# Two steps moved in the outputs stage of a mixture-of-experts kernel: one sum on VectorE, one small projection on TensorE

## The chip, the cores and the metric

The kernel runs on one core of a Trainium2 chip. The engines named here are TensorE (PE; its weight loads are listed apart, as PEld), VectorE (DVE), ScalarE (ACT), GpSimd (POOL) and SyncE (SP), which issues most of the DMAs. Each takes its instructions in the order of its queue and waits for the others at semaphores. The metric is the device time of one execution in microseconds (us), the median of several.

## The reference

Eight sequences `x` of 512 tokens with 256 channels, a context of 64 rows and one anchor row for each sequence. All in fp32.

```python
nx = _layer_norm(x, ln_gamma, ln_beta)
q = nx @ Wq;  k = prototype_bank @ Wk;  v = prototype_bank @ Wv
weights = softmax(einsum('bth,bph->btp', q, k) * H ** (-0.5))
evidence = einsum('btp,bph->bth', weights, v)
combined = concatenate([nx, evidence, anchor], axis=-1)
router_probs = softmax(combined @ router_W + router_b)
h = silu(einsum('btc,ecr->bter', combined, e_w1) + e_b1)
expert_out = einsum('bter,erh->bteh', h, e_w2) + e_b2
routed = sum(expert_out * router_probs[..., None], axis=-2)
g = sigmoid(silu(combined @ gate_w1 + gate_b1) @ gate_w2 + gate_b2)
return x + g * (routed @ out_w + out_b)
```

There are three experts with 512 hidden channels each. `prototype_bank` is the context and `anchor` the broadcast anchor row.

## The kernel before

The eight sequences are worked in four pairs `j` = 0 to 3. A pair goes through `gate_layer` (the first layer of the gate), `expert_layer` for each of the three experts (the first layer of the experts) and `outputs` (the second layer of the gate, then that of the experts). The order of the instructions on each engine is the order in which the program writes them; no scheduler changes it. Work for the next pair is put into this order at named points: the main loop fills the dictionaries `within` and `between` with steps, and `run(point)` in a stage calls the steps of that point.

The products are arranged after Strassen's scheme: the two sequences of a pair and two blocks of channels are the 2 x 2 blocks, and seven products with sums and differences of blocks stand in for eight. So an operand is often a difference that VectorE makes in place, and a result is added up from several PSUM banks. A product is 128 x 512 in fp32 and is listed as two matmuls. `product` (L796) issues it; `experts` issues six of them, one for each pair of hidden blocks, into one bank.

`outputs(j)` begins with the gate. Its products stand in this order on PE: `u` (L1032), `z` (L1033), `y` (L1038), `u` (L1039), `z` (L1043), `u` with `t3` (L1045). In the traces their banks are `ps_gu`, `ps_gz` and `ps_gy`. After the third, fifth and sixth, `gate` adds a bank to a part kept earlier (L1025, VectorE) and takes the sigmoid (L1027, ScalarE). The parts are copied out of the banks by L1035, L1036 and L1040 on ScalarE; the last of these is the copy of `u` that must be done before the sixth product writes on into `u`.

Then `run("begin")` (L1047) calls the steps for the next pair, where there is one: loads of `x`, `transpose_blocks` (L628 on VectorE, the scaling L570 on ScalarE), `value_weights(j + 1, E)`, which multiplies `v` by the gate's and router's part of the first layer (four small matmuls of L771 into `ps_vw`, and the copy L778 to `vw` on ScalarE), `store_router_rows` (L415) and `spread_router_rows` (L423), four DMAs of POOL's queue that pass the router's rows of `vw` through DRAM. `weigh(j, 99)` multiplies the last hidden blocks by the router's probabilities (L880) and takes their differences (L876), on VectorE. `run("gate")` loads the next xg through SP's queue (L475).

Four bias sums follow (L1077 on ScalarE, L1082 on VectorE), and then the second layer of the experts:

- `experts(u, a(q, 0, 0))`, the last gate product L1143 and `keep(r11, u)`. `keep` adds a bank to a result (L1088, VectorE).
- `experts(z, combo(S1), 0, 1)`, the fifth product set in Strassen's count, into the bank `z`.
- `subtract((0, 1), ...)` and `subtract((0, 0), ...)`: two sets of three differences (L1072, VectorE, 128 x 1024 each). The first set overwrites what the product set before it read.
- `keep(r22, z)`, then `run("P5")` with the transposes of the next pair's second block.
- `experts(u, combo(S2), 0, 1)`, the sixth set, which reads the first set of differences, and `keep(r12, u)`.
- In pairs 0 to 2: the product set into `y` (finished by L1102), the next pair's scores (`ps_s`, L649), the set that reads the second differences, and `experts(z, combo(S4), 1, 1)`. In pair 3 the S4 set comes directly after the S2 set, into the same bank `z`.

Of the kernel before, what the change touches and what calls it, by code (L numbers as in the profile page):

```python
# [16 lines left out]
def kernel(  # L17
# [55 lines left out]
    E, C3, RH = e_w1.shape  # L73
# [24 lines left out]
    def bank(i, name):  # L98
        return psum.tile([P, 512], F32, tag=f"b{i}", name=name)
# [117 lines left out]
    S1, S2, S4 = range(3)  # L217
# [576 lines left out]
    def product(ps, lhsT, rhs, start=False):  # L794

        nc.tensor.matmul(ps, lhsT, rhs, start=start, stop=True, skip_group_check=not start)  # L796
# [211 lines left out]
    def outputs(j, steps):  # L1008
        last = j == NP - 1

        def run(point):
            for step in steps.get(point, ()):
                step()
# [9 lines left out]
        def gate(k, i, src, part=None):  # L1023
            if part is not None:
                nc.vector.tensor_tensor(hg[k][i], src, part, ALU.add)  # L1025
                src = hg[k][i]
            nc.scalar.activation(hg[k][i], src, AF.Sigmoid, bias=gb2_c[:, k : k + 1])  # L1027
# [3 lines left out]
        u, z, y = (bank(i, f"ps_g{n}_{j}") for n, i in (("u", 0), ("z", 2), ("y", 4)))  # L1031
# [9 lines left out]
        finish_odd(j, PAIRS[-1])  # L1041
        gate(0, 0, g1, y)
        product(z, gw2s[:, S4, :], b22)  # L1043
        gate(0, 1, g2, z)
        product(u, gw[1][0], t3)  # L1045
        gate(1, 1, g22, u)
# [10 lines left out]
        def experts(ps, lhs, k, i, start=False):  # L1057
            for q in range(NQ):
                product(ps, lhs(q), hidden(j, q, k, i), start=start and q == 0)

        def combo(s):
            return lambda q: w2s[:, s, q, :]

        def subtract(dst, other):

            (k, i), (k2, i2), (k3, i3) = dst, *other
            for e in range(E):
                d, p, m = (
                    S["h", ii, e].rearrange("p (q k) t -> p q k t", k=2)[:, :, kk, :]
                    for kk, ii in ((k, i), (k2, i2), (k3, i3))  # L1070
                )
                nc.vector.tensor_tensor(d, p, m, ALU.subtract)  # L1072

        def bias_sum(role, i, row):

            r = work.tile([P, T], F32, tag=role, name=f"{role}_{j}", bufs=1)
            nc.scalar.activation(  # L1077
                by_side(r), pb[:, row, :, 1, :], AF.Identity, bias=b2o[:, i, 0:1],
                scale=b2o[:, i, 1:2],
            )  # L1080
            for e in range(2, E):
                nc.vector.scalar_tensor_tensor(  # L1082
                    by_side(r), pb[:, row, :, e, :], b2o[:, i, e : e + 1], by_side(r), ALU.mult, ALU.add
                )
            return r

        def keep(r, ps):
            nc.vector.tensor_tensor(r, r, ps, ALU.add)  # L1088
# [38 lines left out]
        def finish_tokens(r, ps, i, row):  # L1127
# [9 lines left out]
        r11, r22, r12, r21 = (  # L1137
            bias_sum(f"r{i + 1}{row + 1}", i, row) for i, row in ((0, 0), (1, 1), (0, 1), (1, 0))
        )
        ug = u  # L1140
        u, y, z = (bank(i, f"ps_{n}2_{j}") for i, n in ((1, "u"), (3, "y"), (5, "z")))
# [4 lines left out]
        run("P1")  # L1146
        experts(z, combo(S1), 0, 1, start=True)
        subtract((0, 1), ((1, 1), (0, 1)))
        subtract((0, 0), ((0, 1), (0, 0)))
        keep(r22, z)  # L1150
        run("P5")
        experts(u, combo(S2), 0, 1)
        keep(r12, u)
# [58 lines left out]
    with tc.manual_schedule(engines=None):  # L1212
# [62 lines left out]
        for j in range(NP):  # L1275


            within, between = {}, {}

            def put(where, n, step, *args):  # L1280
                where.setdefault(n, []).append(lambda: step(*args))
# [44 lines left out]
            if j + 1 < NP:  # L1326
                b0, b1 = 2 * j + 2, 2 * j + 3
                if j + 2 < NP:
                    put(between, "begin", load_x, b0 + 2)
                    put(between, "begin", load_x, b1 + 2)  # L1330
                put(within, (0, "A" if j else "D"), statistics, b0, 0, NT)
                if j == 0:
                    put(within, (0, "D"), statistics, b1, 0, NT)
                for i in range(2):
                    put(within, (0, "D") if j else (1, "S"), deviation, j + 1, i)
                for b in (b0, b1):
                    put(within, (1, "W" if j else "S"), normalize, b)
                    put(within, (1, "W" if j else "S"), store_x, b)
                put(within, (1, "C"), regroup_x, b0)
                put(within, (1, "A" if j else "B"), router_part, b0)  # L1340
                put(within, (1, "D" if j else "B"), router_part, b1)
                put(between, "begin", transpose_blocks, b0)
                put(between, "gate", regroup_x, b1)
                put(between, "begin", value_weights, j + 1, E)
                put(between, "begin", store_router_rows, j + 1)
                put(between, "begin", spread_router_rows, j + 1)
                put(between, "P5", transpose_blocks, b1)
                put(between, "P2", scores, j + 1)
                put(between, "P2", combine_x, j + 1, nc.gpsimd)
                put(between, "P7", softmax, j + 1)  # L1350
                put(between, "P7", value_weights, j + 1, 0)
                put(between, "P7", router_logits, j + 1)
                put(between, "P3", turn_weights, j + 1)
                put(between, "P3", router_exp, j + 1)
            gate_layer(j, within)
            for e in range(E):
                expert_layer(j, e, within)
            outputs(j, between)


# [32 lines left out]
```

## Time and profile before

| what | value |
|---|---|
| median of 3 runs | 463.61 us (463.35 to 463.65) |
| the profiled execution | 463.56 us |
| its span, first to last instruction | 461.4 us |
| PE / DVE / ACT / POOL busy | 456.7 / 364.7 / 214.8 / 100.0 us |
| granted TensorE clock, mean | 0.999 |
| outputs stage of pair 0, 1, 2, 3 begins | 95.9, 202.0, 307.9, 413.8 us |

Busy times are sums over the span. PE's are modelled from pipelined matmuls, so the starts of successive matmuls say more than their lengths: while PE is never kept waiting, two matmuls of 512 columns start 0.43 us apart. Where PE waits for an operand, the wait is listed at the weight load in front of the matmul. The chain of work that ended last is followed back from the last instruction; what is on it sets the time.

### The profile page before, as it was taken

The page shows a single profiled execution, that of the slowest core. Times are in us where ns is not written, and L with a number is a line of the kernel's source. Part 1 is how long each engine was busy: PE and PEld are TensorE (multiplying, and loading weights), DVE is VectorE, ACT ScalarE, POOL GpSimd, SP SyncE. Part 2 cuts the span into 40 slices and gives each one's busy share as a digit, 9 for nine tenths or more (in the row PEclk, how much of TensorE's full clock was granted, in tenths as well). Part 3 has the DMA queues.
Part 4 walks back from the last instruction along what each step waited for, and adds up shares of the span by engine and source line. Part 5 has one row for each costly group of instructions (what it writes and reads, how often), then busy time and mean ns, then how long its engine had stood idle before and what let it go on. Part 6 is the DMA issues. An engine that isn't in the chain of part 4 may idle for free.

```text
span 461.4 us, 4756 instructions
## 1 busy us (share of the span) xinstructions
PE 456.7 (99%) x1457; PEld 210.5 (46%) x1457; DVE 364.7 (79%) x682; ACT 214.8 (47%) x371; POOL 100.0 (22%) x149
## 2 busy tenths in 40 slices
PE   9999999999999999999999999999999999999996
PEld 7544555444444444444444444444444444444455
DVE  2988979969799669869799659878889625797983
ACT  3445683655222666557221576448221456458000
POOL 6357715001181300001072300001062300000020
PEclk9999999999999999999999999999999999999999
DMA  8975587302013326812012235702011570000014
GB/s 282 371 153 135 100 229 124 78 0 46 7 23 45 78 85 137 159 24 46 6 23 30 41 136 116 114 0 46 6 24 23 80 197 0 0 0 1 0 20 71
DMA packets 119400, 35.26 MB, mean 76 GB/s; under 512 B 106044, under 2 KB 116336, under 8 KB 118864
## 3 DMA queue, kind: packets, MB, share of 16 engines
q1 hardware_dynamic: 115168, 26.95, 28.7%
q0 software_dynamic: 2176, 7.17, 4.6%
q10 hardware_dynamic: 2032, 0.85, 0.7%
q8 instruction: 11, 0.18, 0.2%
q14 instruction: 13, 0.11, 0.1%
HBM read 27.56 MB, written 7.39 MB: 76 GB/s over the span
## 4 chain that ended last, share of the span: by engine, by line
PE 95%; DVE 4%; issue 0%
PE ps_u L796 43%; PE ps_z L796 18%; PE ps_y L796 14%; PE ps_vw L771 5%; PE ps_gu L796 3%; PE ps_w2o L501 2%; PE ps_s L649 2%; PE ps_gz L796 1%; DVE h L1072 1%; PE ps_tokens L796 1%; PE ps_wake L294 1%; DVE h L880 1%; PE ps_v L339 1%; PE ps_m L339 1%; PE ps_gy L796 1%; DVE r L1082 0%
## 5 line engine op out<-in xcount | busy, mean ns | idle before, releaser
L880 DVE TENSOR_TENSOR h<-h,pb 128x512 f32<-128x512 f32 x96 | 61.9, 694 | 6.5 <-ACT h L829 6.5
L796 PE MATMUL ps_u<-h,w2o 128*128 128x512 f32 x144 | 64.1, 595 | 0.0
L829 ACT ACTIVATE h<-h,abias 128x512 f32<-128x512 f32 x72 | 49.6, 719 | 12.5 <-DVE h L835 12.0
L796 PE MATMUL ps_u<-nxT,w 128*128 128x512 f32 x112 | 55.3, 604 | 0.0
L796 PE MATMUL ps_z<-wT,vw 64*128 64x512 f32 x104 | 49.5, 605 | 0.0
L1105 POOL TENSOR_TENSOR yb<-yb,xb 128x512 f32<-128x512 f32 x14 | 17.7, 1266 | 143.3 <-DVE yb L1104 114.8
L796 PE MATMUL ps_z<-h,w2s 128*128 128x512 f32 x96 | 42.6, 593 | 0.2 <-DVE r L1088 0.2
L838 ACT COPY h<-ps_u 128x512 f32<-128x512 f32 x48 | 27.9, 582 | 30.2 <-PE ps_u L796 29.8
L796 PEld LDWEIGHTS ps_u<-h,w2o 128*128 128x128 f32 x144 | 27.0, 190 | 32.5 <-issue 29.4
L415 POOL DMA_DIRECT2D vrd<-vw x8 | 5.0, 628 | 137.0 <-ACT vw L778 137.0
L1072 DVE TENSOR_TENSOR h<-h,h 128x1024 f32<-128x1024 f32 x24 | 34.3, 1482 | 0.0
L796 PEld LDWEIGHTS ps_u<-nxT,w 128*128 128x128 f32 x112 | 20.2, 190 | 29.4 <-issue 24.2
L829 ACT ACTIVATE h<-ps_u,abias 128x512 f32<-128x512 f32 x24 | 16.5, 687 | 29.7 <-PE ps_z L796 29.4
L796 PEld LDWEIGHTS ps_z<-h,w2s 128*128 128x128 f32 x96 | 18.2, 190 | 23.5 <-issue 21.8
L796 PE MATMUL ps_z<-T,ws 128*128 128x512 f32 x56 | 28.6, 592 | 0.0
L796 PE MATMUL ps_y<-nxT,w 128*128 128x512 f32 x56 | 28.6, 592 | 0.0
L835 DVE TENSOR_TENSOR h<-h,ps_y 128x512 f32<-128x512 f32 x24 | 16.4, 683 | 15.0 <-PE ps_y L796 14.0
L796 PE MATMUL ps_u<-wT,vw 64*128 64x512 f32 x56 | 27.8, 612 | 0.0
L796 PE MATMUL ps_y<-wT,vw 64*128 64x512 f32 x56 | 27.0, 597 | 0.0
L771 PE MATMUL ps_vw<-w,vT 128*128 128x512 f32 (+1 forms) x64 | 26.9, 543 | 0.0
L796 PE MATMUL ps_u<-T,ws 128*128 128x512 f32 x56 | 26.7, 594 | 0.0
L835 DVE TENSOR_TENSOR h<-h,ps_z 128x512 f32<-128x512 f32 x24 | 16.2, 684 | 13.3 <-PE ps_z L796 13.2
(235 smaller groups left out, 803.2 us busy)
## 6 DMA issues: line engine op xcount, KB each, us to landing
pb<-pd POOLq DMA_DIRECT2D x4, 1536.0 KB, 6.5
xb<-in_x_dram SPq DMA_DIRECT2D x64, 64.0 KB, 2.4
out_dram<-yb SPq DMA_DIRECT2D x56, 64.0 KB, 2.0
w<-in_L_xcond_e_w_dram SPq DMA_DIRECT2D x6, 512.0 KB, 10.2
x<-in_x_dram SPq DMA_DIRECT2D x24, 128.0 KB, 3.2
xd<-x SPq DMA_DIRECT2D x24, 128.0 KB, 2.4
xg<-xd SPq DMA_DIRECT2D x48, 64.0 KB, 2.4
scr_wa<-in_L_xcond_e_w_dram SPq DMA_DIRECT2D x3, 512.0 KB, 12.8
```

What stands on the lines that cost most here:

```text
L339: nc.tensor.matmul(ps, w_sb[:, k, m * P : (m + 1) * P], src[:, k, :], start=(k == 0), stop=(k == KH - 1))
L415: nc.gpsimd.dma_start(S["vrd", j][i].rearrange("e c -> c e"), S["vw", j][row_half(i), R0:])
L501: nc.tensor.matmul(ps[:, d * H : (d + 1) * H], w2T[:, k, (i + d) * P : (i + d + 1) * P], ow_sb[:, k, :], start=(k == 0), stop=(k == KH - 1),)
L649: nc.tensor.matmul(ps[side(i, h), g * NH : (g + 1) * NH], mr[:, k, 2 * j + i, g * TB : (g + 1) * TB], S["nxT", 2 * j + i][:, k, h * NH : ( ...
L771: nc.tensor.matmul(ps, vT[:, k, j * 2 * CT : (j + 1) * 2 * CT], w1[:, KH + k, n0:n1], start=(k == 0), stop=(k == KH - 1),)
L796: nc.tensor.matmul(ps, lhsT, rhs, start=start, stop=True, skip_group_check=not start)
L829: nc.scalar.activation(h, h if src is None else src, AF.Silu, bias=abias[:, c, 2 * j + i : 2 * j + i + 1])
L835: nc.vector.tensor_tensor(h, h, part, ALU.add)
L838: nc.scalar.copy(chunk(n, i, d), part)
L880: nc.vector.tensor_tensor(h, h, S["pb", j][:, i, :, 2 * q // RC, :], ALU.mult)
L1072: nc.vector.tensor_tensor(d, p, m, ALU.subtract)
L1105: nc.gpsimd.tensor_tensor(yb, yb, S["xb", 2 * j + row][:, i, :], ALU.add)
```

## The change

Two steps change places, each within `outputs`; no operation is added or taken away. The sum `keep(r22, z)` on VectorE now stands between the two sets of differences and not behind them, in all four pairs. `value_weights(j + 1, E)` is called at a new point `"S4"`, after the gate's fifth product and ahead of its sum, and so before the product with `t3`; before, it was called at `"begin"`, behind that product, the third sum, its sigmoid and the first transposes. On PE the four matmuls of `ps_vw` change places with the product into `ps_gu`. On ScalarE the copy to `vw` moves from behind the two scalings to between the first and the second sigmoid. The router rows' DMAs keep their place in POOL's queue and wait for that copy. In pair 3 there is no next pair, and `"S4"` is empty.

```diff
@@ -1041,6 +1041,7 @@
         finish_odd(j, PAIRS[-1])
         gate(0, 0, g1, y)
         product(z, gw2s[:, S4, :], b22)
+        run("S4")
         gate(0, 1, g2, z)
         product(u, gw[1][0], t3)
         gate(1, 1, g22, u)
@@ -1146,8 +1147,8 @@
         run("P1")
         experts(z, combo(S1), 0, 1, start=True)
         subtract((0, 1), ((1, 1), (0, 1)))
+        keep(r22, z)
         subtract((0, 0), ((0, 1), (0, 0)))
-        keep(r22, z)
         run("P5")
         experts(u, combo(S2), 0, 1)
         keep(r12, u)
@@ -1341,7 +1342,7 @@
                 put(within, (1, "D" if j else "B"), router_part, b1)
                 put(between, "begin", transpose_blocks, b0)
                 put(between, "gate", regroup_x, b1)
-                put(between, "begin", value_weights, j + 1, E)
+                put(between, "S4", value_weights, j + 1, E)
                 put(between, "begin", store_router_rows, j + 1)
                 put(between, "begin", spread_router_rows, j + 1)
                 put(between, "P5", transpose_blocks, b1)
```

## The prediction

> **What bounds the kernel now.** I read the page first, for the busy shares, the granted clock and the chain that ended last.
>
> ```profile
> PE 456.7 (99%) x1457; PEld 210.5 (46%) x1457; DVE 364.7 (79%) x682; ACT 214.8 (47%) x371; POOL 100.0 (22%) x149
> ...
> PEclk9999999999999999999999999999999999999999
> ...
> PE 95%; DVE 4%; issue 0%
> ```
>
> TensorE (PE) is busy for 99% of the span at full clock, and 95% of the chain is its own work. A change that removes no matmul can only move the time by the small holes in PE's queue. The 4% of VectorE (DVE) in the chain says where such holes are. So I next read the chain in order of time, in the last pair's outputs stage.
>
> ```profile
> 428.32 6.81 DVE h L1072 x6
> 435.13 0.61 DVE r L1088
> 435.74 0.04 issue
> 435.78 5.42 PE ps_z L796 x12
> 441.20 5.15 PE ps_u L796 x12
> ```
>
> Here VectorE runs both sets of differences (L1072, six instructions) and then `keep(r22, z)` (L1088), and PE waits for that sum. Then I read the timelines by engine (start, length, what, and in brackets the idle time before it and its releaser). First PE at the gate of pair 0 and of pair 3, and PE in the experts of pair 0:
>
> ```profile
> 99.39 1.02 PE L796 MATMUL ps_gz<-hg,gw2s 128*128 128x512 f32 x2
> 100.25 1.10 PE L796 MATMUL ps_gu<-g_t,gw_sb 128*128 128x512 f32 x2
> 101.19 1.03 PE L771 MATMUL ps_vw<-w,vT 128*128 128x258 f32 x4
> 102.06 5.31 PE L796 MATMUL ps_u<-h,w2o 128*128 128x512 f32 x12
> ...
> 108.07 5.31 PE L796 MATMUL ps_z<-h,w2s 128*128 128x512 f32 x12
> 113.37 5.42 PE L796 MATMUL ps_u<-h,w2s 128*128 128x512 f32 x12
> 118.62 4.88 PE L796 MATMUL ps_y<-h,w2o 128*128 128x512 f32 x11
> ...
> 417.32 1.02 PE L796 MATMUL ps_gz<-hg,gw2s 128*128 128x512 f32 x2
> 418.18 1.10 PE L796 MATMUL ps_gu<-g_t,gw_sb 128*128 128x512 f32 x2
> 419.12 5.31 PE L796 MATMUL ps_u<-h,w2o 128*128 128x512 f32 x12
> ```
>
> A product is two matmuls 0.43 apart, 0.86 us; a set of six experts is 5.15. Then PE's weight loads, which is where its waits sit; a load normally starts 0.43 before its matmul:
>
> ```profile
> 113.36 0.30 PEld L796 LDWEIGHTS ps_u<-h,w2s 128*128 128x128 f32 x2 [0.81 <-DVE h L1072]
> 218.94 0.19 PEld L796 LDWEIGHTS ps_u<-h,w2s 128*128 128x128 f32 x1 [0.24 <-DVE h L1072]
> 324.83 0.19 PEld L796 LDWEIGHTS ps_u<-h,w2s 128*128 128x128 f32 x1 [0.24 <-DVE h L1072]
> 435.78 0.30 PEld L796 LDWEIGHTS ps_z<-h,w2s 128*128 128x128 f32 x2 [1.02 <-DVE r L1088]
> ```
>
> And VectorE from the last gate sum (L1025) to the first difference:
>
> ```profile
> 101.39 0.69 DVE L1025 TENSOR_TENSOR hg<-g_r,ps_gu 128x512 f32<-128x512 f32 x1 [0.18 <-PE ps_gu L796]
> 112.09 3.49 DVE L1072 TENSOR_TENSOR h<-h 128x1024 f32<-128x1024 f32 x3
> ```
>
> The reader should see one link between them. PE's sixth product set (`experts(u, combo(S2), 0, 1)`) starts on the first difference. In pair 0 it waits for it already; in pairs 1 and 2 its load has the ordinary 0.24 ahead of it but names DVE, so the difference came just in time. From 101.39 to 113.31 VectorE runs 18 instructions back to back, none but the first with an idle time before it: whatever delays the first delays the difference.
>
> **What a late operand costs PE.** Three waits of before give the rule. In pair 0 the load came at 113.36 in place of 112.79 (0.57 late) and the product set that follows started at 118.62 in place of 108.07 + 2 x 5.15 = 118.37: 0.25 lost. In pair 3 the load came at 435.78 in place of 435.00 (0.78 late), and the next set at 441.04 in place of 430.28 + 10.30 = 440.58: 0.46 lost. The gate product of L1045 (`gu`), which waits until L1040 has copied its bank, lost 0.08 in pair 3 with its load at 418.16 in place of 417.75, 0.41 late. So the loss is the lateness less 0.32, which is the lead of the load.
>
> **Part 1, the sum moved (`keep(r22, z)` between the two sets of differences).** It adds and removes nothing: one sum of 0.60 pitch (0.68 long) changes places with three differences of 1.14 pitch. In pairs 0 to 2 it needs the bank of the fifth product, whose last matmul ends at 113.38, and VectorE arrives there at 115.5: no wait is added. The second set ends 0.6 later, near 119.6 in pair 0; PE first reads it with the product set at 125.73, 6 us on, so 0. The transposes of the next x block (L628, 119.51) and `keep(r12, u)` come at the same time as before, since the sum is the same. With the cover of 6 us gone it would cost the 0.6. In pair 3 the order of products is another: `experts(z, combo(S4), 1, 1)` stands directly behind the sixth set and needs this sum. The first three differences end at 431.7, so the sum ends at 432.3 instead of 435.73, ahead of the load's natural 435.00. The hole of 0.46 goes: **-0.46**. Next in line is PE itself, since `keep(r12, u)` ends at 436.3, before the product at 440.58, and sums, stores and the tail behind it follow PE and move with it. Its bounds are 0 and -0.46.
>
> **Part 2, value_weights moved ahead of the product with t3 (pairs 0 to 2; pair 3 has no next pair).** PE gets the four small matmuls (`ps_vw`, 102.06 - 101.19 = 0.87) one product sooner. PE's sum of work is unchanged.
> - Gain on PE: `gu`'s load no longer waits for the copy of L1040, because 0.87 of other work stands before it. From `gz` to `ps_u` pair 3 takes 419.12 - 417.32 = 1.80 where two products are 1.72: 0.08 for each of three pairs.
> - Copy of `vw` on ScalarE: 0.35 long, from behind two scalings (L570) to between the first and the second sigmoid. ScalarE is busy from 100.07 to 109.73 either way, and the scalings and the four bias sums (L1077) stay where they are, at about 104.9 and 106.2, with operands from VectorE at 103.6 and 104.2. 0.
> - The router rows on POOL's queue: two stores (L415) and two loads (L423) start some 2.5 us sooner. They are read first at 139.14 (L709) and were issued by 116.0, so nothing is gained, and no other POOL work stands behind them before the output of the stage. SP's loads of the next xg start after the transposes of L628, 0.86 later, for transposes at 119.5, where landing takes at most 8.2. 0.
> - **The cost.** The third gate sum (`gate(1, 1, g22, u)`) waits for `gu`'s product and heads VectorE's strict order; everything to the differences is queued behind it. It was released at 101.39, 2.00 after `gz`'s start, and in pair 3 also 2.00 after (419.32). For the gate sum after an undelayed product the trace has 1.13 from its first matmul (417.32 to 418.45); 0.86 + 1.13 = 1.99, so PE's wait of 0.08 did not hold it. With `vw` between, it comes 0.86 + 0.87 + 1.13 = 2.86 after `gz`: 0.86 later. Counting from PE's recorded matmul starts (0.87 less the 0.08 saved) it would be 0.79. I take **0.86** and keep 0.79 and 0.87 as ends, as the release is VectorE's own row.
>
> Then PE, pair by pair. Pair 0: the difference ends at 113.31 + 0.86, the load follows at 114.22, natural is 112.79 - 0.08 = 112.71; 1.51 late, 1.19 lost, of which 0.25 was lost before: 1.19 - 0.25 - 0.08 = **+0.86**. Pairs 1 and 2: the first difference starts at 217.64 and 323.53 and takes 1.22, so the loads come at about 219.77 and 325.66 in place of 218.86 and 324.75; 0.91 late, 0.59 lost, less 0.08: **+0.51** each. The later differences come every 1.14, PE needs them every 1.72, so one hole per pair. After it VectorE idles 2.6 to 2.95 before the sum with `ps_y` (L1102), so the delay is not carried on.
>
> Sum: 0.86 + 0.51 + 0.51 - 0.46 = **+1.42 us**. The profiled execution took 463.56 (span 461.4 and about 2.2 around it), 0.05 under the median of 463.61. 463.56 + 1.42 = 464.98, and I say **465.0**. With 0.79 in place of 0.86 it is 464.8; with the hole of pair 3 left as well as the greater delay it is 465.5.
>
> A rule that speaks against the change stands in the Trainium skill, "TensorE: Matmul & The Clock Gate", section "A second HAM failure mode: psum-queue depth-cycling": short idles between groups of matmuls can make the clock gate fall to half rate and back, with windows of about 3.4 us. Worked out from that page, as an estimate, three such windows at half rate would add 3 x 1.7 = 5.1 us, and the sum would be 470.1. The rows here are against it: after the hole at 435.78 the next set still took 5.15, at a granted clock of 0.999 over the run.
>
> **The rivals.**
> - *The delay never reaches PE (so not slower).* If something other than VectorE's queue set the first difference, a gate sum that is 0.86 later would change nothing there. The gains are left: 0.08 in pairs 1 and 2 (pair 0 waits for the same difference, so its 0.08 is lost again) and 0.46: 463.56 - 0.62 = 462.94. The net is 3 x delay - 1.16, so it decides below a delay of 0.39 at the difference. For it: nothing but the habit of slack. Against it: the unbroken row from 101.39 and the named releaser in three pairs. 0.05.
> - *The delay is eaten in part.* With 0.4 to 0.68 left, the net is 0.0 to 0.9, about 464.1: no difference that can be told. For it: VectorE's release is inferred, and PE's own 0.08 shifts are of that size. Against it: pair 3 shows the same 2.00 without `vw`. 0.16.
> - *The sum blocks VectorE.* If `keep(r22, z)` waited in pairs 0 to 2 for the fifth set in its new place, and the second set of differences and the transposes came late for PE's scores (123.86, with scaled blocks ready at 121.76), each pair would lose more. With the holes above, the fifth set ends 2.1 before VectorE arrives; only if VectorE gained that much would it wait, and the scores still have 2.1. A loss of 1 us in each of three pairs on top of the sum gives 468.0. 0.02.
> - *More is late than the difference,* for example ScalarE's scalings or a stretched DVE row beside POOL's earlier queue work, 0.3 per pair: 465.9. Against it: L880 kept its 0.60 pitch beside POOL's issue at 106.63. 0.05.
>
> **How the numbers follow.** The forecast has 0.72, with its own range 464.6 to 465.4. No change that a measurement of this kernel can tell is within 0.2%, that is 0.93 us, up to 464.54. The forecast case and the two dearer rivals are slower, save about 0.01: 0.78. The partial case, that hundredth and most of the absorbed case (462.94 is 0.14% under the median) make 0.20. Faster by more needs 462.68, which only the absorbed case comes near: 0.02. The range from 464.0 to 465.8 leaves out the absorbed case, some of the partial one and the dear tails, less than 2 in 10.
>
> **What would show it.** Right: `ps_vw` between `gz` and `gu`; the third gate sum 2.86 after `gz` in pairs 0 to 2 and 2.00 in pair 3; the load of the sixth set held by DVE h for about 1.5, 0.9 and 0.9; no hole before the S4 set of pair 3, the sum of L1088 ending near 432 plus the shift. Wrong: the difference in its old place relative to PE, or holes that grow at other places such as the scores or the last tokens.

## The result and the profile after

The changed kernel takes 464.72 us (median of 8 runs, 464.67 to 464.94) against 463.51 before (8 runs, 463.35 to 463.65): +1.21 us, a ratio of 1.0026 with a 95% interval of 1.0017 to 1.0034. The profiled execution took 464.94 with a span of 462.8; most of the others had a span of 462.6. Its gate of pair 0 begins 0.14 later than in the kernel before (95.99 against 95.85), ahead of any changed instruction.

The page of the kernel after, busy shares and then the chain that ended last by engine:

```profile
PE 456.1 (99%) x1457; PEld 209.7 (45%) x1457; DVE 365.1 (79%) x682; ACT 214.9 (46%) x371; POOL 100.2 (22%) x149
...
PE 87%; DVE 9%; DMA 1%; issue 1%; SPq 0%; DVEq 0%; ACT 0%
```

The busy times are those of before within 0.8 us and PE is still "99% busy": the page alone hides the loss. VectorE's share of the chain has grown from 4% to 9%. The timeline of PE in pair 0 and, last two lines, in pair 3 (columns: start, length, what, idle time before it and its releaser):

```profile
99.53 1.02 PE L796 MATMUL ps_gz<-hg,gw2s 128*128 128x512 f32 x2
100.39 1.03 PE L771 MATMUL ps_vw<-w,vT 128*128 128x258 f32 x4
101.26 1.02 PE L796 MATMUL ps_gu<-g_t,gw_sb 128*128 128x512 f32 x2
102.11 5.31 PE L796 MATMUL ps_u<-h,w2o 128*128 128x512 f32 x12
107.27 1.02 PE L796 MATMUL ps_gu<-g_t,gw_sb 128*128 128x512 f32 x2
108.12 5.31 PE L796 MATMUL ps_z<-h,w2s 128*128 128x512 f32 x12
114.29 5.42 PE L796 MATMUL ps_u<-h,w2s 128*128 128x512 f32 x12 [0.86 <-DVE h L1073]
...
432.08 5.31 PE L796 MATMUL ps_u<-h,w2s 128*128 128x512 f32 x12
437.23 5.31 PE L796 MATMUL ps_z<-h,w2s 128*128 128x512 f32 x12
```

The weight load of the product with `t3` in pair 0, first in the kernel before, then in the changed kernel:

```profile
100.22 0.30 PEld L796 LDWEIGHTS ps_gu<-g_t,gw_sb 128*128 128x128 f32 x2 [0.65 <-ACT g_r L1040]
...
101.04 0.41 PEld L796 LDWEIGHTS ps_gu<-g_t,gw_sb 128*128 128x128 f32 x2
```

PE's weight loads before the sixth product set in the changed kernel, pairs 0, 1 and 2:

```profile
114.29 0.30 PEld L796 LDWEIGHTS ps_u<-h,w2s 128*128 128x128 f32 x2 [1.69 <-DVE h L1073]
220.62 0.30 PEld L796 LDWEIGHTS ps_u<-h,w2s 128*128 128x128 f32 x2 [1.08 <-DVE h L1073]
326.95 0.30 PEld L796 LDWEIGHTS ps_u<-h,w2s 128*128 128x128 f32 x2 [1.09 <-DVE h L1073]
```

VectorE, the third gate sum and the first difference of pair 0, and the moved sum of pair 3:

```profile
102.32 0.69 DVE L1025 TENSOR_TENSOR hg<-g_r,ps_gu 128x512 f32<-128x512 f32 x1 [0.97 <-PE ps_gu L796]
...
113.02 3.49 DVE L1073 TENSOR_TENSOR h<-h 128x1024 f32<-128x1024 f32 x3
...
433.45 0.68 DVE L1089 TENSOR_TENSOR r<-r,ps_z 128x512 f32<-128x512 f32 x1
```

The wait of 0.65 before the product with t3 is gone in pairs 0 to 2, and with it the 0.08: `gz` to `ps_u` is 102.11 - 99.53 = 2.58, two products of 0.86 and the projection's 0.87 to within 0.01, where it was 2.67. In its place VectorE waits 0.97 for the third gate sum. From this sum to the first difference it runs 18 instructions in pair 0 and 17 in pairs 1 and 2 (one L880 of 0.60 fewer, which is why only pair 0 was late already in the kernel before), and then the sixth product set waits for the difference in all three pairs. In pair 3 the S4 set follows the S2 set (432.08) after 5.15, without a hole.

The program repeats itself from pair to pair, so a difference of starts says what each pair costs. Each column is the time from the first `ps_gu` matmul of a pair's gate to that of the next pair, read from PE's timelines; the fourth is from that matmul of pair 3 to the first `ps_tokens`.

| kernel | pair 0 | pair 1 | pair 2 | pair 3 | sum against before |
|---|---|---|---|---|---|
| before | 106.15 | 105.89 | 105.89 | 40.00 | |
| after | 106.93 | 106.33 | 106.34 | 39.53 | +1.20 |
| sum alone | 106.15 | 105.89 | 105.89 | 39.54 | -0.46 |
| projection alone | 106.94 | 106.33 | 106.34 | 39.99 | +1.67 |
| projection in two halves | 106.50 | 105.90 | 105.89 | 39.54 | -0.10 |
| projection two products sooner | 106.94 | 106.32 | 106.33 | 39.54 | +1.20 |
| copy alone sooner | 106.15 | 105.89 | 105.89 | 39.54 | -0.46 |
| a transpose done twice | 106.90 | 106.30 | 106.30 | 39.53 | +1.10 |
| transposes ahead, projection as before | 105.89 | 105.90 | 105.89 | 39.54 | -0.71 |
| transposes ahead, projection ahead | 105.81 | 105.81 | 105.81 | 39.53 | -0.97 |

The theory: a first difference that comes late costs TensorE its lateness less a lead of 0.32. The rivals: the four matmuls (or their copy) cost by the place they were moved to, whatever VectorE's queue holds; or the moved sum has its own price in pairs 0 to 2.

### The profile page after: what moved, and what is told of

Same layout as the page of the kernel before. It is cut to its first block, busy times and chain, and to the rows that moved or that the text cites. A ratio compares the mean times of both kernels' runs of the same rounds, so it can differ in the third digit from the quotient of the medians.

```text
span 462.8 us, 4756 instructions
## 1 busy us (share of the span) xinstructions
PE 456.1 (99%) x1457; PEld 209.7 (45%) x1457; DVE 365.1 (79%) x682; ACT 214.9 (46%) x371; POOL 100.2 (22%) x149
## 4 chain that ended last, share of the span: by engine, by line
PE 87%; DVE 9%; DMA 1%; issue 1%; SPq 0%; DVEq 0%; ACT 0%
PE ps_u L796 42%; PE ps_z L796 16%; PE ps_y L796 14%; PE ps_vw L771 5%; PE ps_gu L796 3%; DVE h L880 2%; PE ps_w2o L501 2%; PE ps_s L649 2%; PE ps_gz L796 1%; DMA x<-in_x_dram 1%; DVE r L1083 1%; DVE h L876 1%; PE ps_tokens L796 1%; DVE nxT L628 1%; DVE h L1073 1%
## 5 line engine op out<-in xcount | busy, mean ns | idle before, releaser
L880 DVE TENSOR_TENSOR h<-h,pb 128x512 f32<-128x512 f32 x96 | 61.9, 695 | 6.5 <-ACT h L829 6.5
```

Of the source, the lines that this page charges most:

```text
L880: nc.vector.tensor_tensor(h, h, S["pb", j][:, i, :, 2 * q // RC, :], ALU.mult)
```

## The experiments

**The two parts apart.** First the sum alone, on the kernel before:

```diff
         subtract((0, 1), ((1, 1), (0, 1)))
+        keep(r22, z)
         subtract((0, 0), ((0, 1), (0, 0)))
-        keep(r22, z)
```

> The kernel before with the sum alone moved between the two sets of differences; the value projection stays where it was. Theory (a late first difference costs TensorE its lateness less 0.32 us): pairs 0 to 2 unchanged, the hole before the S4 set of pair 3 gone, -0.46 us, about 463.05. Rival (the sum between the sets costs VectorE and what waits for the second set in pairs 0 to 2): no gain or a loss, 463.5 or more.

Measured: 463.08 us against 463.59, ratio 0.9989 (0.9980 to 0.9998). Pairs 0 to 2 keep their times to 0.01 us, pair 3 gets shorter by 0.46. So the sum has no price of its own in pairs 0 to 2, and the rival that gave it one is out.

Then the projection alone, the same diff undone on the kernel after:

```diff
-        keep(r22, z)
         subtract((0, 0), ((0, 1), (0, 0)))
+        keep(r22, z)
```

> The changed kernel with the sum back behind both sets; only the value projection is moved. Theory: +0.79 in pair 0 and +0.44 in pairs 1 and 2, the hole of pair 3 back, +1.67 us against before, about 465.2. Rival (the moved sum carries part of the loss): less than the +1.2 of both parts together.

Measured: 465.33 against 463.59, +1.74, ratio 1.0036 (1.0023 to 1.0049); by pairs +0.79, +0.44, +0.45. The two parts add up: 1.74 - 0.51 = 1.23, against 1.21 for both.

**Is it the matmuls' place or VectorE's queue?** The changed kernel, with VectorE's two transposes and their scalings moved to where VectorE idles, between the first and the second gate sum:

```diff
-                put(between, "begin", transpose_blocks, b0)
...
+                put(between, "S4", transpose_blocks, b0)
                 put(between, "S4", value_weights, j + 1, E)
```

> The changed kernel with the first block's two transposes and scalings taken from behind the third gate sum to the point S4, ahead of the second gate sum, where VectorE idles. The projection still stands before the product with t3, so the third gate sum is as late as in the changed kernel, but 1.22 us of VectorE's queue behind it are gone. Theory: the first difference ends 0.4 us sooner than in the kernel before, no hole is left in pairs 0 to 2; -0.25 in pair 0, -0.08 in each of three pairs, -0.46 in pair 3: -0.95 us, about 462.55. Rival (the four matmuls cost by their place on TensorE or the copy by its place on ScalarE, whatever VectorE's queue holds): as the changed kernel, about 464.7.

Measured: 462.62 against 463.59, ratio 0.9978 (0.9969 to 0.9987), -0.97. The matmuls stand where they stand in the changed kernel, and the third gate sum is as late. VectorE in pair 0 of this kernel:

```profile
98.85 0.69 DVE L1025 TENSOR_TENSOR hg<-g_r,ps_gy 128x512 f32<-128x512 f32 x1 [2.12 <-PE ps_gy L796]
99.46 1.30 DVE L628 STREAM_TRANSPOSE nxT<-xg 128x512 f32<-128x512 f32 x2
100.68 0.65 DVE L1025 TENSOR_TENSOR hg<-g_r,ps_gz 128x512 f32<-128x512 f32 x1
102.23 0.69 DVE L1025 TENSOR_TENSOR hg<-g_r,ps_gu 128x512 f32<-128x512 f32 x1 [0.90 <-PE ps_gu L796]
...
111.75 3.49 DVE L1073 TENSOR_TENSOR h<-h 128x1024 f32<-128x1024 f32 x3
```

and PE:

```profile
108.03 5.31 PE L796 MATMUL ps_z<-h,w2s 128*128 128x512 f32 x12
113.18 5.31 PE L796 MATMUL ps_u<-h,w2s 128*128 128x512 f32 x12
118.33 5.31 PE L796 MATMUL ps_y<-h,w2o 128*128 128x512 f32 x12
```

The transposes fill the 1.03 between the first two gate sums and hold up the second by 0.11 (100.68 - 99.44 = 1.24 after `gz`, against 1.13). The sum still comes 102.23 - 99.44 = 2.79 after `gz`, but the difference starts at 111.75, and the sets follow each other every 5.15. All three pairs now take 105.81. The place of the matmuls costs nothing where VectorE's queue is short enough. This version takes 0.97 us less than the kernel before, 0.2%.

The counter-test: PE's order as before, VectorE alone made late, by doing the first transpose twice on the kernel with the sum moved.

```diff
         for k in range(KH):
+            if b % 2 == 0 and k == 0:
+                nc.vector.transpose(nxT[:, k, :], xg[:, k, :])
             nc.vector.transpose(nxT[:, k, :], xg[:, k, :])
```

> The kernel of the sum alone (TensorE's order as in the kernel before) with the first transpose of the next pair's first block done twice, 0.61 us more on VectorE ahead of the first difference in pairs 0 to 2. Theory: the lateness alone makes the loss, +0.61 in pair 0 and 0.61 - 0.03 - 0.32 = +0.26 in pairs 1 and 2, less 0.46 in pair 3: +0.67 us against before, about 464.2. Rival (the place of the matmuls makes the loss): as the sum alone, about 463.05.

Measured: 464.97 (464.75 to 465.28) against 463.59, +1.38, ratio 1.0029 (1.0019 to 1.0040). The rival's 463.05 is out: a late difference makes the loss with PE's order untouched. The direction is the theory's, but the size is twice the expected +0.67. VectorE's timeline shows where most of the rest comes from:

```profile
102.24 0.70 DVE L629 STREAM_TRANSPOSE nxT<-xg 128x512 f32<-128x512 f32 x1
102.98 1.30 DVE L630 STREAM_TRANSPOSE nxT<-xg 128x512 f32<-128x512 f32 x2
104.21 2.46 DVE L882 TENSOR_TENSOR h<-h,pb 128x512 f32<-128x512 f32 x4
```

The second transpose writes what the first wrote, and starts 0.74 after it where the next starts after 0.61. PE's load for the sixth set comes 114.36 - 99.64 = 14.72 after `gz` where it came 113.36 - 99.39 = 13.97 after it in the kernel before: 0.75 late and not 0.61. With 0.75 of lateness the theory gives 0.75 + 2 x (0.75 - 0.35) - 0.46 = 1.09, and the pairs show +0.75, +0.41, +0.41 and -0.47, which is 1.10. The other 0.28 of the median lies outside these stretches: in the profiled execution the gate of pair 0 begins 0.25 later than before (96.10). This comes from the start of the kernel, ahead of any changed instruction: at 35.01 a sum of VectorE into `T` (L642, L640 in the kernel before) took 1.18 where it took 0.69, and PE's load of `T` waited 0.81 for it. GpSimd had an operation of its own from 35.00 (L236) that in the kernel before ran from 34.39 to 35.03; whether that slowed the sum was not tested, nor whether the other runs, which spread over 0.5 us, have the same.

**Threshold or proportion?** Half of the projection ahead, half in its old place:

```diff
-                put(between, "S4", value_weights, j + 1, E)
+                put(between, "S4", value_half, j + 1)
+                put(between, "begin", value_rest, j + 1)
```

`value_half` issues the matmuls of the first 128 channels, `value_rest` those of the other 128 and the copy.

> The changed kernel with the projection cut in two: the matmuls of its first half of the channels stay before the product with t3, those of the second half and the copy go back behind the third gate sum. TensorE has 0.435 us of it ahead of that product in place of 0.87. Theory (lateness less 0.32 of lead): the sum is 0.435 - 0.08 = 0.36 late; +0.36 in pair 0, 0.36 - 0.03 - 0.32 = 0.01 and so nothing in pairs 1 and 2, -0.46 in pair 3: -0.1 us against before, about 463.5. Rival (the loss grows in proportion to the work put ahead): half of the 1.74 of the projection alone, less 0.46: +0.4, about 464.0.

Measured: 463.35 against 463.56, ratio 0.9997 (0.9988 to 1.0006). The interval doesn't exclude no change, but it leaves out the rival's 1.0009 and the pairs decide: +0.35, +0.01, 0. In pair 1 the load waits 0.65, 0.41 more than the ordinary 0.24, and the pair takes 105.90, 0.09 more than without any hole: as much as the product with t3 gains.

```profile
219.50 0.30 PEld L811 LDWEIGHTS ps_u<-h,w2s 128*128 128x128 f32 x2 [0.65 <-DVE h L1088]
```

So half the work ahead costs less than half: there is a lead, and only what exceeds it counts.

**What the projection brings by itself.** The transposes ahead, the projection behind the product with t3:

```diff
         product(z, gw2s[:, S4, :], b22)
+        run("S4")
         gate(0, 1, g2, z)
...
-                put(between, "begin", transpose_blocks, b0)
+                put(between, "S4", transpose_blocks, b0)
```

(with the sum moved, as in the first diff)

> The sum moved, the projection in its old place behind the product with t3, and the first block's two transposes ahead of the second gate sum. Theory: the difference is 1.2 us sooner, the hole of pair 0 (0.25) and that of pair 3 (0.46) go, the 0.08 before the product with t3 stays in all pairs: -0.71 us, about 462.9; behind the kernel with the projection ahead as well by 0.24. Rival (the projection costs wherever it stands ahead): at or below the 462.6 of that kernel.

Measured: 462.80 against 463.56, -0.76, ratio 0.9985 (0.9976 to 0.9994). Beside the -0.97 with the projection ahead that is 0.21 behind, near the expected 0.24; the pairs show it as 105.89 or 105.90 against 105.81, three times. The runs of the two kernels overlap by 0.04 us, so it is the pairs that carry this.

**The copy's place, and two products instead of one.** The point S4 behind the product with t3:

```diff
-        run("S4")
         gate(0, 1, g2, z)
         product(u, gw[1][0], t3)
+        run("S4")
         gate(1, 1, g22, u)
```

> The changed kernel with the point S4 behind the product with t3 and ahead of the third gate sum: TensorE's order is that of the kernel before, only ScalarE's copy to vw comes sooner, between the second and the third sigmoid. Theory: the copy's place costs and brings nothing, as the sum alone: about 463.05. Rival (the copy ahead of the sigmoids and scalings delays ScalarE's bias sums and what waits for them): above 463.5.

Measured: 463.14 against 463.56, ratio 0.9991 (0.9982 to 1.0000); pairs as with the sum alone. And the point S4 one product sooner:

```diff
         gate(0, 0, g1, y)
+        run("S4")
         product(z, gw2s[:, S4, :], b22)
-        run("S4")
         gate(0, 1, g2, z)
```

> The changed kernel with the projection one product sooner still, ahead of the gate's fifth product, so that the second and the third gate sum are both late. Theory: only the third heads the queue to the first difference, and it is as late as in the changed kernel: about 464.75, the same. Rival (each product it passes costs): about 1.7 more than the changed kernel has over the sum alone, about 466.5.

Measured: 464.81 against 463.56, ratio 1.0027 (1.0017 to 1.0038), the pairs as in the changed kernel to 0.01. Here two gate sums are late. PE's last two gate products and VectorE's sums behind them:

```profile
100.27 1.02 PE L796 MATMUL ps_gz<-hg,gw2s 128*128 128x512 f32 x2
101.13 1.02 PE L796 MATMUL ps_gu<-g_t,gw_sb 128*128 128x512 f32 x2
...
101.40 0.69 DVE L1025 TENSOR_TENSOR hg<-g_r,ps_gz 128x512 f32<-128x512 f32 x1 [1.90 <-PE ps_gz L796]
102.19 0.69 DVE L1025 TENSOR_TENSOR hg<-g_r,ps_gu 128x512 f32<-128x512 f32 x1
```

The second one's delay is taken out of VectorE's idle time; the third starts 102.19 - 98.54 = 3.65 after the gate's fourth product (`u`, L1039), as in the changed kernel (102.32 - 98.67). So neither the copy's place nor the number of products passed has a price. What counts is when the last of the three sums lets VectorE go on.

## Why the prediction was right

Forecast +1.42, measured +1.21. The mechanism is the forecast one, a late gate sum that comes back to PE as a late difference; one term of the sum was too large. By its own steps:

- *The sum moved:* -0.46 forecast; -0.47 in the changed kernel and -0.46 alone. The moved sum of pair 3 ends at 433.45 + 0.68 = 434.13; less the shift of the sixth set (432.08 - 430.28 = 1.80) that is 432.33, where 432.3 was forecast. Nothing in pairs 0 to 2, as forecast.
- *0.08 for the product with t3:* it shows in pairs 1 and 2 when the difference is in time: 105.89 to 105.81.
- *The lateness of the third gate sum:* this is the term that was mis-sized. The prediction took 0.86 by the release of a gate sum 1.13 after its product's first matmul, and kept 0.79, counted from PE's starts, as the low end. Measured is 102.32 - 99.53 = 2.79 after `gz` where the forecast had 2.86, against 2.00 before: 0.79, in all three pairs. What failed is the argument that PE's wait of 0.08 did not hold the sum before. It measured the release behind another product: 1.13 holds for `gz` and `gy`. Behind the product with `t3` the release comes 102.32 - 101.26 = 1.06 after the first matmul when PE doesn't wait, and 1.14 in the kernel before, where it waits 0.08 (101.39 - 100.25). So the 0.08 was part of the old 2.00, and the delay is 0.87 - 0.08 = 0.79. With the projection two products sooner it is the same: 102.19 - 101.13 = 1.06, and 101.40 - 100.27 = 1.13 for `gz`. Why the two products differ by 0.07 stays open.
- *The lead of 0.32:* pairs 1 and 2 cost +0.44 and +0.45 in place of 0.51, pair 0 +0.78 in place of 0.86. The lead itself holds: the loads above waited 1.69, 1.08 and 1.09, so 1.45, 0.84 and 0.85 beyond the ordinary 0.24, and in pair 0 the set after it begins at 119.55 in place of 108.12 + 10.30 = 118.42, 1.13 lost, 0.32 less than the lateness. With 0.79 the prediction's formula gives 0.79 + 0.44 + 0.44 - 0.46 = 1.21. That this meets the measured difference to 0.01 is in part luck: the runs of one kernel spread over 0.3.
- *One hole per pair and nothing carried on:* VectorE idles 2.60 before the sum with `ps_y` in each of pairs 0 to 2, and the pairs' periods add up to the whole.
- *ScalarE's copy, the router rows, the loads of xg:* priced at nothing; the run with only the copy sooner agrees. That the stores of the router rows were issued 2.5 us sooner (104.14 against 106.63 in pair 0) brought nothing that shows.
- *The rule on idle holes and the clock gate,* Trainium skill, "TensorE: Matmul & The Clock Gate", section "A second HAM failure mode: psum-queue depth-cycling": that section describes a kernel that cycles through PSUM banks in each iteration, where PE idles briefly between its groups of matmuls often enough for the clock to go to and fro, and the window of about 3.4 us stands in Part 1 of the page. This case's trace shows nothing of it, with one hole in some 106 us. After the hole of 0.86 in pair 0 the next set took 114.29 to 119.55, 5.26 with its restart, and the mean granted clock of the run was 1.000. Holes so short and so rare did not lower the clock, and the estimate of 470.1 made from that page did not come.

Of the rivals, the absorbed delay is refuted by the releasers of the three loads above, and the blocked VectorE by the run of the sum alone, in which pairs 0 to 2 keep their times. Of more that is late nothing shows: the lateness of the loads less 0.32 accounts for what each pair costs to 0.02. Part of the delay was absent, 0.07 of 0.86; only below 0.70 would the change have fallen within 0.2%.

## What to carry to other kernels

An engine that is 99% busy still waits for others at a few operands; before moving work ahead on it, follow the first result that gets later through the strict queue of the engine that takes it, to the operand that comes back. If that queue runs back to back to the operand, the whole delay comes back, less the lead that the weight load has, here 0.32 us. The remedy can be on the other engine: moving 1.22 us of transposes into VectorE's idle time turned the same two moves from +1.21 to -0.97 us. Of the -0.97 the moved sum has 0.46 and the projection 0.08 in each of three pairs; the rest is to 0.02 the hole of pair 0 (0.25), which the transposes' new place closes by itself.

## What the runs showed of the hardware that was not expected

- A transpose that overwrites the output of the one just before it started 0.74 us after it, where a transpose into another half started 0.61 after. The kernel before has the same step where a VectorE sum reads what the one just before it wrote: L1103 starts 124.69 - 123.97 = 0.72 after L1102, which takes 0.69. In both the next instruction starts only after the one before it has ended, as far as these two cases show.
- The third gate sum followed the first matmul of its product by 1.05 to 1.06 wherever PE didn't wait, and by 1.14 to 1.15 wherever the product waited 0.08 for L1040, in all ten traces; the second gate sum followed its own product by 1.12 to 1.13 wherever VectorE stood idle, also directly behind the small matmuls of 258 columns. A release read behind one product was 0.07 off for the next, as much as the whole gain that was looked for before the product with `t3`.
